# Layer 3 of a four-layer graph network: one of four sums over weights made by an accumulating transfer, weights made ten tiles ahead, a place of its own for the 13th pair

## The chip, the cores and the metric

The kernel runs on one core of one Trainium2 chip. The metric is the device time of an execution in microseconds. Before the change three runs took 2294.19, 2295.3 and 2300.17 us; their median is 2295.3 us.

## What is computed

The input is x (3327 rows of 256 numbers) and a 0/1 matrix adj (3327 by 3327). Four layers follow each other, each with a residual and a layer norm. Layer 3 is three attention layers in a row, called 3a, 3b and 3c here:

```python
def _gat_layer(h, adj, W, a):
    Wh = h @ W
    f1 = Wh @ a[:F_out]
    f2 = Wh @ a[F_out:]
    e = jax.nn.leaky_relu(f1 + f2.T, ALPHA)
    att = jnp.where(adj > 0, e, NEG_INF)
    att = jax.nn.softmax(att, axis=1)
    h_prime = att @ Wh
    return jax.nn.elu(h_prime)
...
h = input @ W0
h = _gat_layer(h, adj, W1, a1)
h = _gat_layer(h, adj, W2, a2)
h = _gat_layer(h, adj, W3, a3)
```

After them x = layernorm(x + h). All arithmetic is in 32-bit floats.

## The kernel before

The 3327 rows are padded to 3328: NT = 26 tiles of 128. The rows whose attention is computed are taken in NB = 7 blocks, six of 512 and one of 256. For one block the kernel runs over the 26 tiles of keys. For each tile it makes a 128 by 512 array of unnormalised weights, and TensorE multiplies these with the values of the tile, adding into PSUM.

**Weights.** In layer 3 (`Gat.weights`) a tile's weights need one ScalarE instruction (`re`, L787) and one VectorE instruction (L800), which also multiplies with the mask. For the blocks 0 to 5 L800 writes into the buffer FTA, seven groups of two rows of 512 numbers per partition. Three "quad" places of two groups each hold the weights of four tiles. `quad` (L702) hands the places out in turn, and counts seven quads to a block: six of four tiles and one for tiles 24 and 25, the 13th pair. The seventh group of FTA stays unused in layer 3.

**Products.** Two tiles make a pair, and a pair's product is made by Strassen's scheme (in Winograd's form) with seven products instead of eight (`products`, 28 matmuls at L935 for a pair and a block of 512). It needs four sums over the weights, s1 to s4, and four over the values (`tsums`). The sums over the weights are made on VectorE for two pairs at a time by `quad_sums` (L871 s3, L872 s1, L873 s2, L874 s4), each into a buffer of the pool "e", which has nine. The first pairs of block 0 and every 13th pair use `sums` (L883 to L886) instead. The sums over the values are made once (`combine`), stored to memory and fetched again for each block by `fetch_tsum` (L857, issued on SP's queue, three buffers); it is called when the weights of the pair are made.

**Order.** The loop goes over `steps` (layer, block, tile). At step s the weights are made up to `ahead_of`, in layer 3 seven tiles ahead (s + 3 + 4), fewer in block 0. In 3c's block 5 `extra` grows by one at each step from tile 11 on, so that the last block's weights are made early. `ahead` loads the row `u` of the next block (L774) and takes its exponential on ScalarE, from step `begin` on. Only the first steps are held to the written order. After that the order of the instructions on each engine is planned when the program is built; the written order counts as a priority there[...].

**Block start.** A block fills four of five PSUM banks. When a block is through, `joined` (L961 on ScalarE, L967 to L979 on VectorE) puts the seven products together and so frees the banks. The first bank of the next block is the fifth, the others have to come free. `finish` then normalises, transposes by a transfer (`turned`, L993), multiplies with the next layer's matrix (`pproj`, L1239), and in 3a and 3b makes the next layer's scores (L719) and sums over values.

**GpSimd** does little: in `combine` it sets a column of ones (`nc.gpsimd.memset`, L843), and once per layer it takes a maximum over partitions (L736).

Of the kernel before, what the change touches and what calls it, by code (L numbers as in the profile page):

```python
# [8 lines left out]
F32 = mybir.dt.float32  # L9
# [5 lines left out]
ALU = mybir.AluOpType  # L15
# [4 lines left out]
P = 128  # L20
D = 256
H = 128
LA = 2
CH = 512
ALPHA = 0.01
BETA = 1.0 - ALPHA
# [7 lines left out]
def gnn_stack(ctx: ExitStack, tc: tile.TileContext, a: dict, N: int, out: bass.AP):  # L34
# [8 lines left out]
    nc = tc.nc  # L43
    NT = (N + P - 1) // P
    NP = NT * P
    NB = (NP + CH - 1) // CH
    LASTP = N - (NT - 1) * P
    assert LASTP == P - 1

    def bw(b):  # L50
        return min(CH, NP - b * CH)

# [8 lines left out]
    work = ctx.enter_context(tc.tile_pool(name="work", bufs=2))  # L61
# [4 lines left out]
    def bank(name):  # L66
        return ps_b.tile([P, CH], F32, tag="pb", name=name)

# [14 lines left out]
    n = 8  # L83
# [19 lines left out]

    FTA = big.tile([P, NB, 2, CH], F32, name="ft")
    FT = [FTA[:, g] for g in range(NB)]
    QUADS = [FTA[:, 2 * r : 2 * r + 2].rearrange("p g h c -> p (g h) c") for r in range(3)]
# [196 lines left out]
    def load_xT(g):  # L303
        wd = bw(g)
        xT = work.tile([P, 2, CH], F32, tag="x4k", name="xT", bufs=2)
        src = a["xT"].rearrange("(h p) n -> p h n", p=P)
        if g == 0:
            for q, c in ((nc.scalar, 0), (nc.sync, D)):
                q.dma_start(xT[:, :, c : c + D], src[:, :, c : c + D])
        else:  # L310
            nc.sync.dma_start(xT[:, :, :wd], src[:, :, g * CH : g * CH + wd])
        xTs[g] = xT
# [108 lines left out]
    def mask(b, j, n=1):  # L421
        wd = bw(b)
        return masks[b][:, j * wd : (j + n) * wd]
# [183 lines left out]
    def by_pairs(L, b, p):  # L607
        return L.key == "2" and b < NB - 1 and p in (KPAIRS if b > 0 else (5, 7, 8, 10))
# [24 lines left out]
    def pair_weights(b, p):  # L633
# [38 lines left out]
        nc.vector.tensor_tensor(x[1][:, :D], c22, m45[:, :D], add)  # L672
        nc.vector.tensor_tensor(c22, c22, m45[:, D:], add)
        yield weights(1)
        m3 = two((s4, b22))
        nc.vector.tensor_tensor(c12, c12, m3[:, :D], add)  # L676
        yield weights(0)

    def weights2(b, j):
# [18 lines left out]

    def quad(i, b, j):
        return QUADS[((i * NB + b) * 7 + j // 4) % 3]  # L702

    class Gat:
        def __init__(self, key):
# [78 lines left out]
        def weights(self, b, j):  # L784
            wd = bw(b)
            t_ = work.tile([P, CH], F32, tag="a", name="re", bufs=4)
            nc.scalar.activation(  # L787
                t_[:, :wd],
                self.u[b][:, :wd],
                AF.Relu,  # L790
                bias=self.nrh[:, j : j + 1],
                scale=self.th[:, j : j + 1],
            )
            if self.quads and b < NB - 1:
                e = quad(self.quads, b, j)[:, j % 4, :]
            elif self.last and b == NB - 1:
                e = V[0][j]
            else:
                e = work.tile([P, CH], F32, tag="e", name="e", bufs=9)
            nc.vector.scalar_tensor_tensor(  # L800
                e[:, :wd],
                t_[:, :wd],
                self.rh[:, j : j + 1],
                mask(b, j),
                ALU.add,
                ALU.mult,
            )
            return e
# [6 lines left out]
    def strassen(L, b):  # L815
        if L.key == "0":
            return 0 < b < NB - 1
        if deep(L):
            return b < NB - 1
        return L.key == "2"  # L820

    def deep(L):
        return L.i > 2
# [3 lines left out]
    kept = {("0", 0): 1, ("0", 1): 1, ("0", 2): 1}  # L827
# [27 lines left out]
    def fetch_tsum(key, b, p):  # L855
        t = work.tile([P, 4 * H + 1], F32, tag="tsum", name="tsums", bufs=3)
        nc.sync.dma_start(t, t_d[key][p])  # L857
        tsums[b, p] = t
# [1 line left out]
    def two_slots(name):  # L860
        return [work.tile([P, 2, D], F32, tag="e", name=name, bufs=9) for _ in range(2)]

    def quad_sums(v):

        e11, e21, e12, e22 = (
            v[:, :, k, h * D : (h + 1) * D] for k in range(2) for h in range(2)
        )
        s3, s1, s2, s4 = (
            work.tile([P, 2, D], F32, tag="e", name="qsum", bufs=9) for _ in range(4)
        )  # L870
        nc.vector.tensor_tensor(s3, e11, e21, ALU.subtract)  # L871
        nc.vector.tensor_tensor(s1, e21, e22, ALU.add)  # L872
        nc.vector.tensor_tensor(s2, s1, e11, ALU.subtract)  # L873
        nc.vector.tensor_tensor(s4, e12, s2, ALU.subtract)  # L874
        return [tuple(x[:, a] for x in (e11, e12, e22, s1, s2, s3, s4)) for a in range(2)]

    def sums(b, e1, e2):

        hw = bw(b) // 2
        s3, s1, s2, s4 = (x[:, i, :hw] for x in two_slots("ssum") for i in range(2))  # L880
        e11, e21 = e1[:, :hw], e1[:, hw : 2 * hw]
        e12, e22 = e2[:, :hw], e2[:, hw : 2 * hw]
        nc.vector.tensor_tensor(s3, e11, e21, ALU.subtract)  # L883
        nc.vector.tensor_tensor(s1, e21, e22, ALU.add)
        nc.vector.tensor_tensor(s2, s1, e11, ALU.subtract)
        nc.vector.tensor_tensor(s4, e12, s2, ALU.subtract)  # L886
        return e11, e12, e22, s1, s2, s3, s4
# [593 lines left out]
    steps = [(L, b, j) for L in layers for b in range(NB) for j in range(NT)]  # L1481
    made = deque()

    pairs = {}

    def make(s):
        if s >= len(steps):
            return
        L, b, j = steps[s]
        make_weights(L, b, j)  # L1490
        if j % 2 and by_pairs(L, b, (j + 1) // 2):
            pairs[b, j + 1] = pair_weights(b, (j + 1) // 2)
            next(pairs[b, j + 1])

    cells = {}

    def in_quad(b, j):
        return j < NT - 2 and (b > 0 or j > 3)

    def make_weights(L, b, j):  # L1500
        if strassen(L, b) and j % 2 == 0 and kept.get((L.key, j // 2)) != b:
            fetch_tsum(L.key, b, j // 2)
        if by_pairs(L, b, j // 2):
            made.append(next(pairs[b, j - j % 2]))
            if j % 2:
                e1, e2 = made.pop(), made.pop()
                made.append(None)
                made.append(sums(b, e1, e2))
        else:
            if L.is_gat:  # L1510
                made.append(L.gat.weights(b, j))
                if deep(L) and strassen(L, b) and in_quad(b, j):
                    made[-1] = cells.setdefault((L.i, b, j // 2), []) if j % 2 else None
                    if j % 4 == 3:
                        v = quad(L.gat.quads, b, j).rearrange("p (a k) c -> p a k c", k=2)
                        for a_, x in enumerate(quad_sums(v)):
                            cells.pop((L.i, b, j // 2 - 1 + a_)).extend(x)
                    return
            else:
                made.append((weights0 if L.key == "0" else weights2)(b, j))  # L1520
            if strassen(L, b) and j % 2:
                e2, e1 = made.pop(), made.pop()
                made.append(None)
                made.append(sums(b, e1, e2))
# [15 lines left out]
    for part in (k0, q0, k0, q0, q0, k0, k0, q0, q1):  # L1540
        next(part, None)
    make(0)
    next(q1)
    make(1)
    prep = iter(())
    kprep = iter(())
# [3 lines left out]

    upto = LA
    extra = 0
    ends = deque()

    def make_to(n):
        nonlocal upto
        while upto < n:
            make(upto)
            upto += 1

    for s, (L, b, j) in enumerate(steps):
        last = L.key == "3c"
# [10 lines left out]
        if first:  # L1573
# [6 lines left out]
            elif j % 4 == 3 and j < 16:  # L1580
                load_xT((j + 9) // 4)
        ahead_of = s + LA + 1
        if deep(L):
            ahead_of += 4 if b else min(4, j // 3)
            if b == 0 and pending:
                ahead_of = max(s + LA + 1, min(ahead_of, L.i * NB * NT + NT - 2))
            if not last:
                end_of = (L.i + 1) * NB * NT
                ahead_of = max(s + LA + 1, min(ahead_of, end_of))
        make_to(ahead_of + extra)  # L1590
        if first:
            if j < 2:
                next(q1)
# [19 lines left out]
        if end:  # L1613

            k, h = divmod(2 * j, NT)
            for i in (h, h + 1):
                for o in range(2 if k else 1):
                    e = made[i][:, k * P : (k + 1) * P]
# [43 lines left out]
        if s == 3:  # L1662
            start.__exit__(None, None, None)
        if L.key == "0" and j == NT - 1 - LA:
            asum = sum_adj(b)
# [24 lines left out]
            nl, nb = (None if last else layers[L.i + 1]), 0  # L1690
        begin = 14
        if deep(L) and b < NB - 1:
            begin = 2 if last and b == NB - 2 else 10
        if L.key == "1" and (b, j) == (0, 22):
            sum_weights(w[L.w])
        if L.key == "2" and b * NT + j in KSTEPS:
# [91 lines left out]
```

## Time and profile before

| | value |
|---|---|
| median of three runs | 2295.3 us |
| the profiled execution, its own time | 2298.3 us |
| its span, first to last instruction | 2296.5 us |
| TensorE's granted clock, mean | 0.996 |
| ScalarE's L787, all | 728 instructions, 777 ns each |
| VectorE's L800 into ft | 468 instructions, 740 ns each |
| VectorE's L871, L872, L873, L874 | 105 each, 681 ns median |
| TensorE's L935 from tsums and qsum | 2520 records, 277 ns each |
| transfers, total | 286.13 MB, mean 125 GB/s |

The profile comes from one execution, which took 2298.3 us where the median of the runs is 2295.3. A long name such as `po<-tsums,qsum` says what is written and from what. A matmul in 32-bit floats leaves two records. Matmuls overlap, so their mean durations are longer than the steps from one to the next; the same holds for VectorE, where a row's 681 ns stand for about 0.60 us from start to start in the timeline. A wait is put down to the release that the profile saw last, which is not always the operand that was really missing.

Layer 3 begins at about 1368 us, where L800 writes its first ft (1369.6 us), and lasts to the end.

### The profile page before, as it was taken

How to read it: one execution, taken by the hardware profiler on the slowest of the kernel's cores; microseconds unless marked ns; L12 is line 12 of the kernel's file. 1: busy time of each engine (PE TensorE's matmuls, PEld its weight loads, DVE VectorE, ACT ScalarE, POOL GpSimd, SP SyncE). 2: the span in 40 equal slices, each digit the busy share in tenths (PEclk: the TensorE clock that was granted, in tenths of full speed). 3: DMA queues.
4: the chain of work that ended last, by engine and by line, in shares of the span. 5: the costliest groups of instructions: out<-in, count | busy, mean ns of one | idle time of the engine just before them, and what ended most of it. 6: DMA issues, size and time to landing. Idle time of an engine off the chain costs nothing.

```text
span 2296.5 us, 41597 instructions
## 1 busy us (share of the span) xinstructions
PE 2253.7 (98%) x15183; PEld 2004.9 (87%) x15183; DVE 1982.4 (86%) x5407; ACT 1239.4 (54%) x2012; POOL 41.6 (2%) x196
## 2 busy tenths in 40 slices
PE   9999999999999999999999999999999999999997
PEld 7788887888888877888888899999999999999997
DVE  7789999866777777898898889899799998899996
ACT  4667777764555423223233245666666665665763
POOL 0000001000000000000000000000000000000000
PEclk9999999999999999999999999999999999999999
DMA  8655565523222322132132254454444544355542
GB/s 277 196 177 177 188 193 188 162 84 90 77 72 55 106 62 80 56 100 81 56 100 71 74 176 127 131 151 130 122 122 143 136 143 137 95 165 155 154 120 56
DMA packets 186207, 286.13 MB, mean 125 GB/s; under 512 B 80413, under 2 KB 105492, under 8 KB 181396
## 3 DMA queue, kind: packets, MB, share of 16 engines
q1 hardware_dynamic: 185732, 283.22, 41.2%
q8 instruction: 120, 1.97, 0.4%
q14 instruction: 83, 0.68, 0.1%
q10 hardware_dynamic: 272, 0.26, 0.1%
HBM read 228.21 MB, written 38.44 MB: 116 GB/s over the span
## 4 chain that ended last, share of the span: by engine, by line
PE 75%; DVE 14%; DMA 4%; ACT 4%; issue 2%; POOL 0%; DVEq 0%; SPq 0%; ACTq 0%; POOLq 0%
PE po L935 35%; PE po L1653 16%; PE ps L647 6%; PE ps L511 6%; PE ps L686 5%; DVE ft L800 3%; DMA turned<-planes 2%; PE pproj L1239 2%; ACT re L787 2%; DVE qsum L873 1%; DVE qsum L872 1%; DVE ejunk L719 1%; PE pv L1322 1%; PE pgq L541 1%; DVE qsum L874 1%
## 5 line engine op out<-in xcount | busy, mean ns | idle before, releaser
L787 ACT ACTIVATE re<-u,nrh,th 128x512 f32<-128x512 f32 (+1 forms) x728 | 536.6, 777 | 348.1 <-DVE ft L800 172.9
L1653 PE MATMUL po<-v,e 128*128 128x257 f32 x1872 | 422.3, 381 | 1.0 <-ACT p L1182 0.8
L1653 PEld LDWEIGHTS po<-v,e 128*128 128x128 f32 x1872 | 353.0, 190 | 60.5 <-issue 9.8
L935 PE MATMUL po<-tsums,qsum 128*128 128x128 f32 (+1 forms) x2520 | 353.9, 277 | 15.8 <-ACT re L787 9.2
L800 DVE SCALAR_TENSOR_TENSOR ft<-re,rh,mask 128x512 f32<-128x512 f32 x468 | 339.1, 740 | 16.1 <-ACT re L787 14.2
L935 PEld LDWEIGHTS po<-tsums,qsum 128*128 128x128 f32 x2520 | 317.2, 193 | 19.1 <-ACT re L787 12.8
L935 PE MATMUL po<-tsums,ssum 128*128 128x128 f32 (+1 forms) x2082 | 292.5, 276 | 3.8 <-DMA tsums<-t3a_d 1.9
L935 PE MATMUL po<-v,ft 128*128 128x129 f32 x1872 | 287.6, 277 | 4.1 <-DVE p L975 3.4
L935 PEld LDWEIGHTS po<-tsums,ssum 128*128 128x128 f32 x2082 | 262.3, 192 | 6.3 <-DMA tsums<-t3a_d 2.3
L935 PEld LDWEIGHTS po<-v,ft 128*128 128x128 f32 x1872 | 252.9, 193 | 9.7 <-issue 5.0
L935 PEld LDWEIGHTS po<-v,e 128*128 128x128 f32 x1196 | 172.4, 192 | 37.6 <-issue 24.9
L935 PE MATMUL po<-v,e 128*128 128x129 f32 x1196 | 185.1, 275 | 0.0
L800 DVE SCALAR_TENSOR_TENSOR e<-re,rh,mask 128x512 f32<-128x512 f32 (+1 forms) x234 | 148.9, 655 | 38.4 <-PE po L1653 28.3
L524 ACT ACTIVATE ex<-ps,rq 128x512 f32<-128x512 f32 (+1 forms) x183 | 118.8, 652 | 114.8 <-PE ps L511 112.0
L511 PE MATMUL ps<-ft 128*128 128x512 f32 (+1 forms) x364 | 166.9, 564 | 0.0
L496 DVE SCALAR_TENSOR_TENSOR e<-ex,mask 128x512 f32<-128x512 f32 (+1 forms) x182 | 115.4, 648 | 48.9 <-ACT ex L694 31.6
L525 DVE SCALAR_TENSOR_TENSOR e<-ex,mask 128x512 f32<-128x512 f32 (+1 forms) x183 | 116.6, 643 | 32.4 <-ACT ex L524 32.0
L935 PE MATMUL po<-tsums,ft 128*128 128x128 f32 x936 | 143.1, 275 | 0.0
L686 PE MATMUL ps<-gT,ft 128*128 128x512 f32 (+1 forms) x336 | 129.8, 527 | 0.0
L935 PE MATMUL po<-v,qsum 128*128 128x128 f32 x840 | 128.4, 275 | 0.0
L935 PEld LDWEIGHTS po<-tsums,ft 128*128 128x128 f32 x936 | 123.6, 192 | 0.0
L660 ACT ACTIVATE ex<-ex,off 128x512 f32<-128x512 f32 x98 | 67.0, 716 | 101.7 <-DVE ex L676 69.1
(347 smaller groups left out, 3566.0 us busy)
## 6 DMA issues: line engine op xcount, KB each, us to landing
mask<-mask_d SPq DMA_DIRECT2D x30, 1664.0 KB
stage<-in_adj_a SPq DMA_DIRECT2D x78, 512.0 KB
tsums<-t_d SPq DMA_DIRECT2D x152, 256.5 KB
tsums<-t3a_d SPq DMA_DIRECT2D x77, 256.5 KB
tsums<-t3b_d SPq DMA_DIRECT2D x77, 256.5 KB
tsums<-t3c_d SPq DMA_DIRECT2D x77, 256.5 KB
mask_d<-mask SPq DMA_DIRECT2D x6, 1664.0 KB
u<-s_d SPq DMA_DIRECT2D x24, 256.0 KB
```

The costliest lines, as they stand in the source:

```text
L496: nc.vector.scalar_tensor_tensor(e[:, :wd], t_[:, :wd], 0.0, mask(b, j), ALU.add, ALU.mult)
L511: nc.tensor.matmul(ps[:, :wd], FT[j // 4][:, 0, (j % 4) * P : (j % 4 + 1) * P], FT[b][:, 1, :wd], start=True, stop=True,)
L524: nc.scalar.activation(t_[:, c], ps[:, c], AF.Exp, scale=rq[:, j : j + 1])
L525: nc.vector.scalar_tensor_tensor(e[:, c], t_[:, c], 0.0, mask(b, j)[:, c], ALU.add, ALU.mult)
L647: nc.tensor.matmul(ps[:, i * D : (i + 1) * D], l, r, start=True, stop=True)
L660: nc.scalar.activation(x[k], x[k], AF.Exp, bias=off, scale=1.0 / D**0.5)
L686: nc.tensor.matmul(ps[:, :wd], FT[j // 4][:, h, (j % 4) * P : (j % 4 + 1) * P], g[:, h, :wd], start=(h == 0), stop=(h == 1),)
L787: nc.scalar.activation(t_[:, :wd], self.u[b][:, :wd], AF.Relu, bias=self.nrh[:, j : j + 1], scale=self.th[:, j : j + 1],)
L800: nc.vector.scalar_tensor_tensor(e[:, :wd], t_[:, :wd], self.rh[:, j : j + 1], mask(b, j), ALU.add, ALU.mult,)
L935: nc.tensor.matmul(o, x, y, start=(p == 0 and g not in banks[:i]), stop=(p == NT // 2 - 1 and g not in banks[i + 1 :]),)
L1239: nc.tensor.matmul(pm[:, :D], pT[:, h, :], w[L.w][:, h, :], start=(h == 0), stop=(h == 1),)
L1653: nc.tensor.matmul(pos[k], e[:, k * P : (k + 1) * P], V[L.i % 2][i], start=(i == 0), stop=(i == NT - 1),)
```

## The change

Six things are changed, all for 3a, 3b and 3c.

1. `quad_sums` writes s1 over e21, the part of the weights that only s1 and s3 read, instead of taking a fourth buffer. In most quads (all of the blocks 1 to 5, and from tile 15 on in block 0) s1 isn't made on VectorE: GpSimd's queue issues a transfer that adds e22 onto e21 in place. In the other quads VectorE makes it in place.
2. The function becomes a generator. In the queued quads s2 and s4, which need s1, are made only when the weights of three more tiles have been made (`SLACK`, `due`, `make_due`), at the latest with tile 25.
3. `quad` gives tiles 24 and 25 the seventh group of FTA, and the six quads of a block go over the three places in turn.
4. The weights are made s + LA + 9, that is up to ten tiles further than the step's own need, in the blocks from 1 on; in block 0 the lead grows with j // 2 instead of j // 3. In block 5 of each layer and in the last block there are limits of their own.
5. `fetch_tsum` is no longer called with the weights: `fetch_to` calls it at most six tiles ahead of the step.
6. `begin`, the step from which `ahead` runs, goes from 10 to 6.

```diff
-    def quad(i, b, j):
-        return QUADS[((i * NB + b) * 7 + j // 4) % 3]
+    def quad(j):
+        if j >= NT - 2:
+            return FTA[:, NB - 1]
+        return QUADS[j // 4 % 3]
...
-    def quad_sums(v):
+    def quad_sums(v, queued):
...
-        s3, s1, s2, s4 = (
-            work.tile([P, 2, D], F32, tag="e", name="qsum", bufs=9) for _ in range(4)
-        )
+        qsum = lambda: work.tile([P, 2, D], F32, tag="e", name="qsum", bufs=9)
+        s3, s1 = qsum(), e21
         nc.vector.tensor_tensor(s3, e11, e21, ALU.subtract)
-        nc.vector.tensor_tensor(s1, e21, e22, ALU.add)
+        if queued:
+            nc.gpsimd.dma_start(out=s1, in_=e22, accum_op=ALU.add)
+            yield
+        else:
+            nc.vector.tensor_tensor(s1, e21, e22, ALU.add)
+        s2, s4 = qsum(), qsum()
         nc.vector.tensor_tensor(s2, s1, e11, ALU.subtract)
         nc.vector.tensor_tensor(s4, e12, s2, ALU.subtract)
-        return [tuple(x[:, a] for x in (e11, e12, e22, s1, s2, s3, s4)) for a in range(2)]
+        yield [tuple(x[:, a] for x in (e11, e12, e22, s1, s2, s3, s4)) for a in range(2)]
...
+    fetched = 0
+
+    def fetch_to(n):
+        nonlocal fetched
+        while fetched <= min(n, len(steps) - 1):
+            L, b, j = steps[fetched]
+            if strassen(L, b) and j % 2 == 0 and kept.get((L.key, j // 2)) != b:
+                fetch_tsum(L.key, b, j // 2)
+            fetched += 1
...
         L, b, j = steps[s]
+        if not deep(L):
+            fetch_to(s)
         make_weights(L, b, j)
+        make_due(j)
...
+    due = deque()
+
+    def make_due(j):
+
+        if due and j >= due[0][0]:
+            _, (i, b, p), rest = due.popleft()
+            for a_, x in enumerate(next(rest)):
+                cells.pop((i, b, p + a_)).extend(x)
...
-                        v = quad(L.gat.quads, b, j).rearrange("p (a k) c -> p a k c", k=2)
-                        for a_, x in enumerate(quad_sums(v)):
-                            cells.pop((L.i, b, j // 2 - 1 + a_)).extend(x)
+                        v = quad(j).rearrange("p (a k) c -> p a k c", k=2)
+                        queued = b > 0 or j > 11
+                        rest = quad_sums(v, queued)
+                        if queued:
+                            next(rest)
+                        k = min(j + SLACK, NT - 1) if queued else j
+                        due.append((k, (L.i, b, j // 2 - 1), rest))
...
-            ahead_of += 4 if b else min(4, j // 3)
+            far = s + LA + 9
+            plain = (L.i * NB + NB - 1) * NT
+            if b == NB - 2:
+                far = min(far, max(ahead_of + 4 + extra, plain))
+            elif b == NB - 1:
+                far = ahead_of + 4 + extra
+            ahead_of = far if b else min(far, ahead_of + j // 2)
...
-        make_to(ahead_of + extra)
+        if deep(L):
+            fetch_to(min(s + LA + 4, ahead_of - 1))
+        make_to(ahead_of)
...
-            begin = 2 if last and b == NB - 2 else 10
+            begin = 2 if last and b == NB - 2 else 6
```

More of the change, by code (lines that the diff above doesn't have):

```diff
@@ L23 @@
 LA = 2
+SLACK = 3
 CH = 512
@@ L794, in weights @@
             if self.quads and b < NB - 1:
-                e = quad(self.quads, b, j)[:, j % 4, :]
+                e = quad(j)[:, j % 4, :]
             elif self.last and b == NB - 1:
@@ L1500, in make_weights @@
     def make_weights(L, b, j):
-        if strassen(L, b) and j % 2 == 0 and kept.get((L.key, j // 2)) != b:
-            fetch_tsum(L.key, b, j // 2)
         if by_pairs(L, b, j // 2):
```

## The prediction

> **What bounds the kernel now.** I read the page's busy shares first, then busy time by stretch, then the waits of the matmul engine, then the timeline at two block starts, one with a hole and one without.
>
> ```profile
> PE 2253.7 (98%) x15183; PEld 2004.9 (87%) x15183; DVE 1982.4 (86%) x5407; ACT 1239.4 (54%) x2012; POOL 41.6 (2%) x196
> ...
> core 0: us, PE busy (x) PEld busy (x) DVE busy (x) ACT busy (x) POOL busy (x), PEclk, DMA share, GB/s
> 1376.00:2122.00 746.00, 722.30 (x5930) 703.23 (x5928) 691.10 (x1639) 466.75 (x743) 3.67 (x30) 1.00 0.47 135
> 2122.00:2264.00 142.00, 141.56 (x1171) 138.72 (x1172) 135.74 (x335) 90.61 (x138) 0.00 (x0) 1.00 0.47 132
> ```
>
> TensorE is the bound. The change touches only layer 3, about 1368 us to the end. From 1376 to 2122 us TensorE stands 746.0 - 722.3 = 23.7 us; in the last blocks of 3c (2122 to 2264) it stands 0.4 us. The prize is therefore some 24 us, 1% of the span, unless the matmuls themselves change, and the diff leaves all of them.
>
> ```profile
> PE po L935 <- ACT re L787: 9.2, 7, 2.4
> PE po L935 <- DVE p L975: 3.4, 6, 1.0
> PE po L935 <- DMA tsums<-t3a_d: 2.3, 3, 1.5
> PE po L935 <- DVE zs L970: 2.2, 1, 2.2
> PE po L935 <- issue: 2.2, 2, 1.9
> ...
> 1603.82 0.61 PE L935 MATMUL po<-v,ssum 128*128 128x128 f32 x4
> 1604.27 0.83 PE L935 MATMUL po<-v,ft 128*128 128x129 f32 x6
> 1607.53 0.77 PE L935 MATMUL po<-tsums,qsum 128*128 128x128 f32 x2 [2.43 <-ACT re L787]
> ...
> 1605.69 0.68 DVE L872 TENSOR_TENSOR qsum<-ft 128x512 f32<-128x512 f32 x1
> 1606.30 0.15 DVE L967 COPY zs<-po 128x2 f32<-128x2 f32 x1
> 1606.41 0.69 DVE L873 TENSOR_TENSOR qsum<-qsum,ft 128x512 f32<-128x512 f32 x1
> ...
> 1607.15 0.28 DVE L973 TENSOR_TENSOR p<-p,po 128x128 f32<-128x128 f32 x1
> ...
> 2208.57 0.83 PE L935 MATMUL po<-v,ft 128*128 128x129 f32 x6
> 2209.24 1.06 PE L935 MATMUL po<-tsums,qsum 128*128 128x128 f32 x8
> ```
>
> The waits name ACT re, but the operand had been ready for long. Six matmuls of the new block go into the fifth PSUM bank, the seventh needs a bank of the old block, and it starts at 1607.53, just after L973 of joined() (the first ends at 1607.43) has read that bank. So the hole is VectorE and ScalarE coming late to joined(): L967 starts 2.0 us after the new block's first matmul. At 2208.57 it was early (VectorE's L967 at 2208.17 in the timeline) and there is no hole. Adding up the holes of the timeline between 1372 and 2265 us that stand at such block starts (2.23, 1.47, 0.81, 2.43, 1.67, 1.62, 1.44, 2.77, 1.87, 0.87, 0.23) gives 17.4 us; the rest is 4.5 us at layer starts and the last blocks, 1.1 us of tsums fetches and small ones.
>
> Why is VectorE late? From 1588.75 to 1607.7 it works almost without a pause (0.6 us), and its row of weights (L800) is bound by places: block 5 of 3a starts its first weight at 1593.89, when the matmuls of tiles 16 to 19 are through in block 4, because pair 13 takes a whole quad place and the third place back is theirs. That is six tiles before the block start; its weights, the sums of the quads and the follow-up of hidden layers all fall into the same 10 us.
>
> **What the Trainium skill says.** "DMA: Bandwidth & Descriptors", section "SWDGE vs HWDGE vs iDMA": an accumulating transfer can be issued from GpSimd alone, its descriptors written in software. Section "Anatomy of one DMA — SWDGE (gpsimd) path": about 2.0 us fixed plus bytes over 436 GB/s; for 256 KB an estimate of 2.6 us, for a plain copy. The trace has no GpSimd transfer; its nearest rows are SP's: a 256.5 KB store issued at 1589.70 releases VectorE at 1593.68 (4.0 us), a 256 KB load of u issued at 1581.78 releases ScalarE at 1585.07 (3.3 us), and tsums pieces in the chain of waits run up to 8.05 us beside a mask load. "SBUF — State Buffer", section "Who interferes with whom": tensor_tensor has no two-port mode and does not lock GpSimd's writes out; no run so far shows it.
>
> **The change part by part.**
> - *Sum by transfer.* Per layer, queued quads are 5 blocks x 6, and j = 15, 19, 23 of block 0: 33, in three layers 99. Each takes an L872 off VectorE, 681 ns long, 0.60 us from start to start: 99 x 0.60 = 59 us of VectorE, 3.6 us per block. Of the stretch between 1588.75 and 1607.43 three L872 go (1588.75, 1599.97, 1605.69): 1.8 us of the 2.4 us hole. Elsewhere the time buys nothing, as TensorE is the bound.
> - *What it adds.* 99 transfers of 256 KB on GpSimd's queue, 26 MB on top of 286 (the destination is read as well). The DMA engines are 0.47 busy, so it is room enough on average; beside a mask load (one per block) it is late. GpSimd is 2% busy; ahead of a transfer in its queue can stand the memset of the ones column (L843), which waits for an x4k place, but the VectorE subtraction behind the same place waits as well.
> - *The added wait.* s2 waits for the landing. Behind it on VectorE's queue stand weights, other sums and, at a block start, joined(), for which TensorE waits within 0.7 us. Three tiles later is 3 x 0.66 = 2.0 us if VectorE runs flat out and 3 x 1.56 = 4.7 us at TensorE's pace. Latency unknown: bounds 2.6 us (the page) and 8 us (the longest piece above); I take 4.5 us, the store's 4.0 plus something for the read of the destination. Then the landing is in time at TensorE's pace and late by up to 2.5 us in a burst. The instruction order is planned with a modelled latency (L852 of one pair stands between two sums of another), so other work will stand in most of these gaps. A mean stall of 0.5 us would cost 99 x 0.5 = 50 us of VectorE, less than the 59 removed; a gain below nothing is not excluded and is the rival below.
> - *Place for pair 13, ten tiles ahead.* Six quads over three places: quad 0 of the next block follows quad 3 and starts ten tiles ahead of the block start instead of six, 4 x 1.56 = 6 us earlier. It spreads the burst and makes room for late sums: +0 to -5 us, counted with the holes. The mask is no obstacle: it is issued at 1586.37 for a block whose weights start at 1643.50, just after the last weight of two blocks earlier (1585.59) has freed its buffer. u is loaded from step 6 instead of 10, which the lead needs; its 3.3 us lie beside matmuls.
> - *One place of nine less per quad* (s1 lies in e21) and the two DVE sums of block 0 in place: 0.
> - *fetch_to.* tsums are fetched at most six tiles ahead, and three buffers allow no more anyway (SP waits for po 428 us in L857 now): 0, without it the lead would block SP's queue. With 3a's first pairs fetched from step 0 on: +0 to 1.5 us (a hole of 1.5 us on tsums is there now).
> - *Last block.* Its weights come later in program order; VectorE does them from 2232.97 on, with nothing else urgent: 0 to +1 us.
>
> Sum: three quarters of the 17.4 us at block starts, -13; half of 2.5 us of holes on sums elsewhere, -1; new waits at some of 18 block starts, +3: -11 us. What is late next is the PSUM bank itself: ScalarE's copy (0.35), L967 to L973 (0.4) against six matmuls (0.67), and the 3c blocks show this fits. The profiled execution took 2298.3 us (span 2296.5) and becomes 2287; the median of the runs, 2295.3, becomes 2284.
>
> **The rivals.**
> - *A: holes stay.* In 3c (2122 to 2264) VectorE is busy 95.6% and TensorE does not stand; before 2122 it is busy 92.6% and TensorE does. So it may be order, not load: ScalarE's weights ahead of its copy L961 (1605.86, behind one at 1605.14), or the wait for the transposed tile on ScalarE (2.55 us at 1575.72). Then a fifth of the 17.4 goes: -3 us, 2292. Against it: from 1588 on VectorE has no pause.
> - *B: slower, VectorE stands at the head of its queue for the accumulate.* Its place: s2 (L873), 99 times. VectorE's spare per quad is the 0.6 us removed and 0.4 us of today's idle (746 - 691 = 55 us over about 80 queued quads is 0.7, part of it unusable). It decides from a latency of about 3.0 (flat out, with another sum between) + 1.0 + 0.5 = 4.5 us if the plan puts nothing else in between, close to what I take; each 0.25 us more costs 99 x 0.25 = 25 us, as TensorE then waits for sums. With 4.75 us: 2320. For it: traffic at 0.47 and loads of up to 8 us. Against: the lead of ten tiles is 15.6 us, and a plan that knows the latency.
> - *C: it doesn't do what it says*: the lead is not reached because re or places are late; then it goes like A.
>
> **How the numbers follow.** Forecast, 2284 (2276 to 2289 by the unknowns): 0.56. A and C, 2292: 0.17. B, 2320 (2296 to 2380): 0.27. No change means within 0.3%, about 7 us, what a measurement of this kernel can tell (2288.4 to 2302.2). Faster: 0.53 of the forecast and 0.03 of A, 0.56; same: 0.03 + 0.14 + 0.02 = 0.19; slower 0.25. The range from 2275 leaves 0.05 out below, and up to 2316 about 0.15 of B above.
>
> **What would show it.** L872 falls from 105 to 6; L873 shows no long wait for a DMA; the stretch that is now 746 us has under 13 us of TensorE idle; the L935 waits for re, p and zs fall from 15 us to under 5; L800 of a block starts ten tiles ahead. Wrong: VectorE idle before L873 on a landing, over 0.5 us a quad, and TensorE waiting for qsum; or joined() still 2 us late with VectorE on time.

## The result, and the profile after

The changed kernel took 2518.0 us, median of four runs (2508.7 to 2528.6); the kernel before, run beside it, took 2294.7 us. The ratio is 1.097, interval 1.092 to 1.102. The forecast was 2284 us, the range ended at 2316 us, and slower had been given 0.25. The profiled execution took 2528.6 us, its span is 2526.8 us; the profile shown of the kernel before has a span of 2296.5 us. Lines have moved: s3 is now L873, the transfer L875, s2 L880, s4 L881, the weights L803 (ScalarE's part L790), the products L942.

The page of the changed kernel, rows of the parts on busy time, slices, queues, groups and transfers:

```profile
PE 2323.2 (92%) x15183; PEld 2066.9 (82%) x15183; DVE 1940.0 (77%) x5308; ACT 1243.3 (49%) x2012; POOL 161.3 (6%) x295
...
PEclk9999999999999999999999998999988989988998
...
q0 software_dynamic: 26928, 25.96, 7.1%
...
L942 PE MATMUL po<-tsums,qsum 128*128 128x128 f32 x1680 | 251.2, 296 | 109.3 <-ACT re L790 60.8
...
L880 DVE TENSOR_TENSOR qsum<-ft 128x512 f32<-128x512 f32 x105 | 72.5, 691 | 258.6 <-DMA ft<-ft 253.0
...
L875 POOL DMA_DIRECT2D ft<-ft x99 | 119.1, 1204 | 744.0 <-DVE qsum L873 343.7
...
ft<-ft POOLq DMA_DIRECT2D x99, 256.0 KB, 4.5
```

The row of s2 and the row of the clock before:

```profile
L873 DVE TENSOR_TENSOR qsum<-qsum,ft 128x512 f32<-128x512 f32 x105 | 71.5, 681 | 0.5
...
PEclk9999999999999999999999999999999999999999
```

VectorE does 42 us less work than before (1940.0 against 1982.4) and the span is 230 us longer. The row of L880 says where: its 105 instructions are busy for 72.5 us, and before them VectorE stood 258.6 us, where it stood 0.5 us before. Of these, 253.0 us ended with the landing of a transfer. The median transfer takes 4.5 us from issue to landing. The row PEclk shows a second loss: the granted clock of TensorE drops in seven of the last sixteen slices.

The same stretches as in the prediction, by busy time:

```profile
core 0: us, PE busy (x) PEld busy (x) DVE busy (x) ACT busy (x) POOL busy (x), PEclk, DMA share, GB/s
1376.00:2122.00 746.00, 621.42 (x4724) 602.07 (x4723) 518.32 (x1230) 375.06 (x598) 82.53 (x93) 0.92 0.53 129
2122.00:2264.00 142.00, 119.45 (x898) 115.36 (x897) 106.46 (x253) 75.61 (x120) 16.16 (x16) 0.92 0.56 139
```

Of 746 us, TensorE stands 125 us (24 before) and VectorE 228 us (55 before). With both idle for so long, neither is the bound: the time goes into a wait that VectorE sits out at the head of its queue. The clock of 0.92 is a mean; the clock record of the trace has full and half speed only.

The difference of the spans, 2526.8 - 2296.5 = 230.3 us, divides on TensorE into 160.8 us of more idle time (203.6 against 42.8, span less busy) and 69.5 us of more busy time (2323.2 against 2253.7) for the same 15183 matmul records.

Where it happens, on VectorE's timeline in 3b (start, duration, engine, line; in brackets the idle time before):

```profile
2010.78 0.69 DVE L873 TENSOR_TENSOR qsum<-ft 128x512 f32<-128x512 f32 x1
2011.38 1.41 DVE L803 SCALAR_TENSOR_TENSOR ft<-re,rh,mask 128x512 f32<-128x512 f32 x2
2015.96 0.69 DVE L880 TENSOR_TENSOR qsum<-ft 128x512 f32<-128x512 f32 x1 [3.18 <-DMA ft<-ft]
...
2019.17 0.68 DVE L873 TENSOR_TENSOR qsum<-ft 128x512 f32<-128x512 f32 x1
...
2024.66 0.41 DVE L1270 SCALAR_TENSOR_TENSOR v<-elu_e,z 128x256 f32<-128x256 f32 x1
2030.06 0.69 DVE L880 TENSOR_TENSOR qsum<-ft 128x512 f32<-128x512 f32 x1 [4.98 <-DMA ft<-ft]
```

On GpSimd's and on SP's queue beside it:

```profile
2011.99 1.20 POOL L875 DMA_DIRECT2D ft<-ft  x1 [5.49 <-DVE qsum L873]
2020.39 1.20 POOL L875 DMA_DIRECT2D ft<-ft  x1 [7.19 <-PE po L942]
```

```profile
2020.54 0.32 SPq L428 DMA_DIRECT2D mask<-mask_d  x1
```

In the first quad shown, s3 is followed on VectorE's queue by two weights (2011.38 to 2012.78) and then by s2. The transfer went out at 2011.99 and landed 4 us later, so VectorE stood 3.18 us. In the second, the last of a block, fifteen other instructions stood between the two, until 2025.1; but the load of the next block's mask (1664 KB) went out 0.15 us after the transfer, and s2 could start only 9.7 us after the issue. Over all 99 transfers the trace gives 3.7 us at least, 4.5 us as the median, 5.4 us as the mean; 16 took over 8 us, up to 11.3. Each of these 16 has a mask load that was issued between 2.0 us before it and 1.2 us after it.

The whole sum can be read from the start and landing times of the 99 transfers. From the end of s3 it takes 0.6 us on average until the transfer is issued and 5.4 us until it has landed. VectorE has 3.4 us of other work there (1.3 to 5.4 us), so about 2.5 us are left, 99 times. The 16 late ones make up 95 us of the stand before s2.

"Perfetto Trace Analysis" in the Trainium skill, section "Tensor Engine Instruction (MATMUL, LD_WEIGHTS)", calls the queues of VectorE and ScalarE strictly first in, first out. The trace agrees for VectorE, as ScalarE's timeline shows:

```profile
2012.16 1.52 ACT L790 ACTIVATE re<-u,nrh,th 128x512 f32<-128x512 f32 x2 [0.41 <-DVE ft L803]
2017.36 0.81 ACT L790 ACTIVATE re<-u,nrh,th 128x512 f32<-128x512 f32 x1 [3.68 <-DVE ft L803]
```

Two more `re` were made by 2013.7, but the weights that use them stood behind s2 and came after 2016.5. ScalarE then stood 3.68 us, until such a weight had freed a place for `re`. So a stall of VectorE is not made good by work done in advance meanwhile: ScalarE stops with it.

What follows on TensorE, from its own timeline:

```profile
2018.92 1.06 PE L942 MATMUL po<-tsums,qsum 128*128 128x128 f32 x8
...
2039.79 0.37 PE L768 MATMUL psr<-ident,sd 128*4 128x128 f32 x1 [6.65 <-DVE sd L722]
...
2053.41 2.05 PE L942 MATMUL po<-tsums,qsum 128*128 128x128 f32 x8 [3.88 <-ACT re L790]
2055.25 0.64 PE L942 MATMUL po<-v,ft 128*128 128x129 f32 x2
2055.68 1.92 PE L942 MATMUL po<-tsums,ft 128*128 128x129 f32 x8
```

TensorE stands 6.65 us for a score that VectorE makes, and 3.88 us at the next block start. Then eight records of the kind that took 1.06 us at 2018.92 take 2.05 us. (Where matmuls are counted, 28 to a pair, the trace's records are meant; the kernel issues 14 for a pair.) "TensorE: Matmul & The Clock Gate" in the Trainium skill, section "Part 1: The HAM clock gate (the "warmup" mystery)", states that after an idle window of about 3.4 us the array runs at half its clock. The trace agrees in part. Its clock record has 32 stretches at half the clock, 195 us of the span, nearly all of 3.4 or 6.8 us; before there were three, 16.8 us. Apart from the stretch at the very end of the kernel, 23 of them began in or just after a gap of TensorE of 3.4 us or more, but eight at gaps of only 1.9 to 3.3 us, and the two before at gaps of 2.2 and 2.4 us. Here the measurement decides: shorter gaps than the page's can be followed by the half clock. TensorE was busy for 137.8 us of these stretches, 6.6 us before. Half of the difference, 66 us, is an estimate of what the slow clock cost, and close to the 69.5 us of additional busy time.

TensorE's waits for fetched sums over values (`tsums`) grow as well, from 2.7 us between 1376 and 2264 us before to 32.2 us.

### The profile page after: what moved, and what is told of

It is laid out like the page before. It is cut to its first block, busy times and chain, and to the rows that moved or that the text cites. A ratio compares the mean times of both kernels' runs of the same rounds, so it can differ in the third digit from the quotient of the medians.

```text
span 2526.8 us, 41544 instructions
## 1 busy us (share of the span) xinstructions
PE 2323.2 (92%) x15183; PEld 2066.9 (82%) x15183; DVE 1940.0 (77%) x5308; ACT 1243.3 (49%) x2012; POOL 161.3 (6%) x295
## 5 line engine op out<-in xcount | busy, mean ns | idle before, releaser
L790 ACT ACTIVATE re<-u,nrh,th 128x512 f32<-128x512 f32 (+1 forms) x728 | 540.4, 778 | 590.6 <-DVE ft L803 337.8
L803 DVE SCALAR_TENSOR_TENSOR ft<-re,rh,mask 128x512 f32<-128x512 f32 x468 | 336.6, 744 | 31.1 <-PE po L942 26.1
L942 PE MATMUL po<-tsums,qsum 128*128 128x128 f32 x1680 | 251.2, 296 | 109.3 <-ACT re L790 60.8
L942 PEld LDWEIGHTS po<-tsums,qsum 128*128 128x128 f32 x1680 | 227.8, 209 | 115.5 <-ACT re L790 62.5
L942 PE MATMUL po<-v,ft 128*128 128x129 f32 x1872 | 302.5, 286 | 3.8 <-DVE p L982 3.0
L942 PE MATMUL po<-tsums,ssum 128*128 128x128 f32 (+1 forms) x2082 | 292.3, 276 | 2.0 <-DVE ssum L892 1.4
L942 PE MATMUL po<-tsums,ft 128*128 128x128 f32 (+1 forms) x1776 | 261.2, 291 | 28.7 <-DMA ft<-ft 26.6
L942 PEld LDWEIGHTS po<-v,ft 128*128 128x128 f32 x1872 | 266.8, 202 | 9.2 <-issue 3.4
L880 DVE TENSOR_TENSOR qsum<-ft 128x512 f32<-128x512 f32 x105 | 72.5, 691 | 258.6 <-DMA ft<-ft 253.0
L942 PEld LDWEIGHTS po<-tsums,ssum 128*128 128x128 f32 x2082 | 262.2, 192 | 4.3 <-DVE ssum L892 2.0
L942 PEld LDWEIGHTS po<-tsums,ft 128*128 128x128 f32 x1776 | 239.2, 207 | 30.9 <-DMA ft<-ft 28.0
L942 PEld LDWEIGHTS po<-v,e 128*128 128x128 f32 x1196 | 172.4, 191 | 37.9 <-issue 24.7
L942 PE MATMUL po<-v,e 128*128 128x129 f32 x1196 | 185.2, 275 | 0.1
L803 DVE SCALAR_TENSOR_TENSOR e<-re,rh,mask 128x512 f32<-128x512 f32 (+1 forms) x234 | 148.9, 655 | 36.7 <-PE po L1691 28.1
L875 POOL DMA_DIRECT2D ft<-ft x99 | 119.1, 1204 | 744.0 <-DVE qsum L873 343.7
L942 PE MATMUL po<-v,qsum 128*128 128x128 f32 x840 | 136.5, 288 | 0.0
```

The costliest lines, as they stand in the source:

```text
L790: nc.scalar.activation(t_[:, :wd], self.u[b][:, :wd], AF.Relu, bias=self.nrh[:, j : j + 1], scale=self.th[:, j : j + 1],)
L803: nc.vector.scalar_tensor_tensor(e[:, :wd], t_[:, :wd], self.rh[:, j : j + 1], mask(b, j), ALU.add, ALU.mult,)
L875: nc.gpsimd.dma_start(out=s1, in_=e22, accum_op=ALU.add)
L942: nc.tensor.matmul(o, x, y, start=(p == 0 and g not in banks[:i]), stop=(p == NT // 2 - 1 and g not in banks[i + 1 :]),)
```

## The experiments

Theory 1 is the mechanism of rival B: s2 waits at the head of VectorE's queue for the landing, and everything behind it waits with it. Against it stood three others: that the order of places, lead and fetches is spoilt (rival 2 in the expectations); that the 26 MB of transfers or their issue disturb other work (rival 3); that the three-tile delay does. The medians and the ratios to runs of the kernel before on the same chip:

| kernel | us | ratio, interval |
|---|---|---|
| e1, all sums on VectorE, rest of the change kept | 2306.3 | 1.0045, 1.0033 to 1.0057 |
| e2, s2 taken from s3, transfers kept | 2314.6 | 1.0078, 1.0066 to 1.0090 |
| e3, the last quad of each block on VectorE | 2420.9 | 1.0540, 1.0523 to 1.0558 |
| e4, five tiles of delay for three | 2397.4 | 1.0432, 1.0412 to 1.0452 |
| e5, kernel before with transfers, s2 from s3 | 2297.2 | 1.0005, 0.9997 to 1.0013 |
| e6, kernel before with transfers and their wait | 2456.5 | 1.0694, 1.0678 to 1.0709 |
| e7, e2 with priority for `joined` | 2315.8 | 1.0088, 1.0074 to 1.0102 |
| e7b, kernel before with priority for `joined` | 2292.0 | 0.9987, 0.9980 to 0.9995 |
| e9, e5 with block 0 on VectorE | 2299.6 | 1.0016, 1.0010 to 1.0023 |
| e10, e9 with priority for `joined` | 2296.1 | 1.0003, 0.9995 to 1.0011 |
| e11, e2 with the old lead and `begin` | 2317.9 | 1.0092, 1.0077 to 1.0108 |
| e12, e5 with the own place for pair 13 | 2316.7 | 1.0092, 1.0078 to 1.0105 |
| e13, e2 without the delay | 2315.5 | 1.0089, 1.0076 to 1.0103 |

### Without transfers (e1), and with transfers that s2 doesn't wait for (e2)

```diff
-                        queued = b > 0 or j > 11
+                        queued = False
```

> The changed kernel, but s1 always made in place by VectorE, no transfer; lead of ten tiles, place for the 13th pair, fetch_to and begin stay. Theory 1 (VectorE stands in its queue at L880 until the accumulate has landed, 253 us in all): the loss is gone, 2285 to 2298 us, no wait of VectorE on a landing of ft. Rival 2 (the new order of places, lead or fetches costs the time): still above 2400 us. Rival 3 (the transfers' traffic or GpSimd's issue costs it): as theory 1 here.

Since s1 = e21 + e22 and s3 = e11 - e21, s2 = s1 - e11 is also e22 - s3. e2 writes it so; only the matmuls read s1 then.

```diff
-        nc.vector.tensor_tensor(s2, s1, e11, ALU.subtract)
+        nc.vector.tensor_tensor(s2, e22, s3, ALU.subtract)
```

> The changed kernel with one operand pair changed: s2 = e22 - s3 instead of s1 - e11, the same number, so that no VectorE instruction needs the transfer; the 99 transfers stay. Theory 1: 2278 to 2300 us, and TensorE alone waits for a landing now and then. Rival 3 (traffic, issue on GpSimd): 2450 us or more. Rival 2: 2450 us or more.

e1 came to 2306.3 us, so nearly all of the loss hangs on the transfers; it is some 8 us above what was expected of it, a remainder that the other parts of the change cost. e2 keeps all 99 transfers and comes to 2314.6 us: 203 of the 223 us are gone with one operand changed. That is 15 us above what was expected, a remainder that is taken up below. The row of s2 and the stretch by busy time in e2:

```profile
L880 DVE TENSOR_TENSOR qsum<-ft,qsum 128x512 f32<-128x512 f32 x105 | 71.9, 685 | 0.8
```

```profile
1376.00:2122.00 746.00, 719.23 (x5903) 698.05 (x5903) 649.27 (x1544) 466.25 (x744) 103.47 (x113) 1.00 0.67 163
```

The idle time before s2 is 0.8 us for 258.6, TensorE is at full clock again, and the DMA engines are busier than in the changed kernel (0.67 against 0.53). TensorE's waits for tsums are back at 1.9 us. In e2, too, 13 of the 99 landings take over 8 us, and no instruction of VectorE waits for them. It was not the traffic, it was who waited for it.

### The collision with the mask (e3) and more cover (e4)

```diff
-                        queued = b > 0 or j > 11
+                        queued = (b > 0 or j > 11) and j < 23
```

> The changed kernel, with the sixth quad of each block (j = 23) left to VectorE: 81 transfers instead of 99. These are the transfers that start within a microsecond of a mask load and land after 9 to 11 us. Theory 1 with the mask as a large part of it: 18 stalls of about 5 us go, 2518 becomes 2420 to 2450 us. If the mask has no special part: a sixth of the loss goes, about 2480 us. Rival 2: no change.

```diff
-                        k = min(j + SLACK, NT - 1) if queued else j
+                        k = min(j + (5 if b else SLACK), NT - 1) if queued else j
```

> The changed kernel with five tiles instead of three between s3 and s2 in the blocks from 1 on: in VectorE's built order 12.2 instructions stand between them on average instead of 7.9. Theory 1: 4.3 x 0.6 = 2.6 us more cover for each transfer, VectorE's wait at L880 falls from 253 us to 60 to 130 us, the time to 2360 to 2430 us. Rivals 2 and 3: 2500 us or more.

The waits of VectorE in e3 and e4 (total, times, longest):

```profile
DVE qsum L880 <- DMA ft<-ft: 159.8, 67, 5.1
```

```profile
DVE qsum L880 <- DMA ft<-ft: 98.6, 38, 7.0
```

With the last quad of each block back on VectorE, 18 of 99 transfers are gone and 97 us with them; no landing takes over 8 us any more. So the sixth quads, a fifth of the transfers, make over 40% of the loss. What is left is as telling: the 81 landings of e3 take 4.5 us on average, and VectorE still stands 159.8 / 81 = 2.0 us for each. With two tiles more of delay the wait falls to 98.6 us in total and the time by 121 us. In the built program, the number of instructions on VectorE's queue between s3 and s2 goes from a mean of 7.9 (most often 2, in 28 of 105 quads) to 12.2. Both came out as theory 1 expected, and both fit a loss that is set by the latency less the work between s3 and s2.

### The transfer in the kernel before, with its wait (e6) and without (e5)

e6 puts `quad_sums`, SLACK and `make_due` into the kernel before and leaves its places, its lead and its `begin`; `fetch_to` comes with it.

> The change's transfer alone: s1 by transfer, s2 after it and three tiles later, but lead, places of the quads and begin as before the change. In VectorE's built order 7.6 instructions stand between s3 and s2 on average, 7.9 in the changed kernel. Theory 1 (VectorE waits in its queue for the landing): nearly the whole loss, 2450 to 2550 us, with 200 us or more of VectorE's wait at s2. If the lead of ten tiles or the places make the waits what they are: under 2400 us.

e5 is the kernel before with its buffers as in the change (s1 in e21) and these lines:

```diff
-        nc.vector.tensor_tensor(s1, e21, e22, ALU.add)
-        nc.vector.tensor_tensor(s2, s1, e11, ALU.subtract)
+        if queued:
+            nc.gpsimd.dma_start(out=s1, in_=e22, accum_op=ALU.add)
+        else:
+            nc.vector.tensor_tensor(s1, e21, e22, ALU.add)
+        nc.vector.tensor_tensor(s2, e22, s3, ALU.subtract)
```

> The kernel before, with s1 by transfer in the same 99 quads and s2 = e22 - s3, so that VectorE waits for no transfer; lead and places as before. It takes 59 us off VectorE and adds the traffic. If the holes at block starts come from VectorE's load (the step of the prediction): 2280 to 2288 us. If they come from the order of the queues: 2293 to 2303 us, with VectorE's share falling to about 87% and TensorE's idle unchanged.

e6: 2456.5 us, 160 us above the kernel before: the waiting transfer alone does most of the harm, and the place and the lead, which were to make room for it, add 61 us to that. The waits of VectorE in e6, then one of its transfers on GpSimd's queue and the mask on SP's:

```profile
DVE qsum L878 <- DMA ft<-ft: 210.5, 89, 7.4
```

```profile
1522.90 1.20 POOL L873 DMA_DIRECT2D ft<-ft  x1 [6.58 <-issue]
```

```profile
1525.41 0.32 SPq L428 DMA_DIRECT2D mask<-mask_d  x1
```

Here the mask load goes out 2.5 us after the sixth quad's transfer, at other blocks mostly 1.2 to 2.5 us after it, and only 3 landings take over 8 us, for 16. The mask's buffer comes free with the weights of tile 25; with a place of its own, pair 13 follows the sixth quad at once, and the mask with it. That is the reading that fits both timelines, and e12 below bears it out.

e5: 2297.2 us, no change. The relief of VectorE does arrive (its share falls to 84%), but not in the time. That is in the range expected if the order of the queues makes the holes, and yet the holes do shrink. The waits of TensorE between 1376 and 2264 us in e5:

```profile
PE po L937 <- DMA ft<-ft: 5.6, 3, 2.0
PE po L937 <- DVE p L977: 3.7, 10, 0.9
PE pproj L1241 <- DVE zlast L1388: 2.5, 1, 2.5
PE po L937 <- ACT re L787: 2.4, 2, 1.3
```

The holes at block starts (re, p) fall to 6 us, where the prediction counted 17.4. Three new ones take 5.6 us: the quad at tile 15 of block 0, once in each layer, where the lead is short and the matmuls reach s1 before it has landed. And the end (the row of zlast, here 2.5 us, 0.8 before) grows: from the start of the last block of 3c to the end e5 takes 46.6 us for 43.4. The span is 3.5 us shorter in the profiled execution (2293.0 against 2296.5); over 13 runs nothing of it is left. Of the two profiled executions, e5's was faster than its median, 2294.7 against 2297.2 us, and the one before slower, 2298.3 against 2295.3 us.

### What the other 20 us are (e12, e11, e13, e7)

e12 is e5 with only `quad` as in the change (three lines); e11 is e2 with the lead and `begin` of before (`fetch_to` stays, at the same distance of six tiles); e13 is e2 with s2 and s4 made at once; e7 is e2 with a priority for `joined`:

```diff
# e11
-            far = s + LA + 9
...
+            ahead_of += 4 if b else min(4, j // 3)
# e13
-                        k = min(j + SLACK, NT - 1) if queued else j
+                        k = j
# e7
-                z = joined(pos, b, p4)
+                with tc.high_priority():
+                    z = joined(pos, b, p4)
```

> e5_before_free (transfer, nobody on VectorE waiting, lead as before) with one part of the change added: the place of its own for the 13th pair, so that a block's first weights can begin ten tiles ahead of it. If this place lets weights stand ahead of joined() and so costs what separates e11 (2318 us) from e5 (2297 us): 2308 to 2318 us. If it is the three tiles' delay of s2 and s4 or the fetches: 2294 to 2301 us.

> e2_s2_from_s3 with the lead, fetches and begin as before the change; the place for the 13th pair stays. e2 is 17 us over e5, which has neither. If the lead of ten tiles (more weights and sums ahead of joined() in the queues) costs it: 2294 to 2302 us. If the place costs it: 2308 to 2316 us.

> e2_s2_from_s3 (transfer, nobody on VectorE waiting, lead of ten tiles, own place) with s2 and s4 made at once instead of three tiles later. If the delay is what costs e2 its 17 us over e5: 2294 to 2301 us. If the place or the lead: 2309 to 2316 us.

> e2_s2_from_s3 with a higher priority for joined() in the planned order, so that fewer weights and sums stand ahead of it on VectorE and ScalarE at a block start. If the place of joined() in the queues makes the holes: 2295 to 2305 us, waits of L942 on re and p under half of the 18 us of e2. If not: 2310 to 2318 us.

Neither the lead (2317.9) nor the delay (2315.5) nor the rank of `joined` (2315.8) moves e2's 2314.6 us. The place alone does: from 2297.2 to 2316.7 us (2296.3 and 2295.8 us for the kernel before beside them). Waits of TensorE between 1376 and 2264 us in e12, and VectorE at one of its block starts:

```profile
PE po L939 <- DVE p L979: 9.0, 13, 0.8
PE po L939 <- DMA ft<-ft: 7.7, 4, 2.2
PE po L939 <- ACT re L789: 5.4, 6, 1.4
PE po L939 <- issue: 4.1, 5, 1.3
```

```profile
1823.93 0.68 DVE L872 TENSOR_TENSOR qsum<-ft 128x512 f32<-128x512 f32 x1
1824.53 0.15 DVE L971 COPY zs<-po 128x2 f32<-128x2 f32 x1
...
1825.38 0.69 DVE L877 TENSOR_TENSOR qsum<-ft,qsum 128x512 f32<-128x512 f32 x1
1825.99 0.41 DVE L978 TENSOR_TENSOR p<-p,po 128x256 f32<-128x256 f32 x1
...
1826.40 0.66 DVE L878 TENSOR_TENSOR qsum<-ft,qsum 128x512 f32<-128x512 f32 x1
1826.98 0.41 DVE L979 TENSOR_TENSOR p<-p,po 128x256 f32<-128x256 f32 x1
```

L971 to L979 are part of `joined`. The sums of a new quad (L872 s3, L877 s2, L878 s4) fall exactly there, one ahead of it and two inside it, and TensorE then waits for L979. The row for p has thirteen such waits, none over 0.8 us: the same hole at nearly every block start from 1521 us on. That makes 12.4 us more at block starts than in e5 (9.0 + 5.4 + 4.1 against 3.7 + 2.4), 2.1 us more for landings, 1.1 us more at zlast, and 3.8 us more of busy matmuls, of 22.3 us between the two spans. With seven quads on three places the phase between quads and block starts changes from block to block; with six on three it is the same in every block, and it is a bad one. That is read from the timeline; no run shifted the phase to prove it, and why e7 did not cure it stays open. Nor did a run put the place alone into the kernel before: in e1, where place, lead, fetches and `begin` of the change stand without any transfer, they cost 9 us together, so part of the 19.5 us comes from place and transfers together.

The place alone also moves the mask load. In e5 the mask load nearest to a transfer mostly goes out 3 to 5 us after it, and no landing takes over 8 us. In e12 it mostly goes out 1.1 us ahead of the transfer, as here, and 10 landings take over 8 us:

```profile
1497.20 0.32 SPq L427 DMA_DIRECT2D mask<-mask_d  x1
1498.31 1.20 POOL L874 DMA_DIRECT2D ft<-ft  x1 [6.93 <-PE po L939]
```

### Looking for a version that gains (e7b, e9, e10)

> The kernel before with a higher priority for joined() alone. If the place of joined() in the queues makes the holes at block starts (17 us): 2283 to 2291 us. If VectorE's load makes them: 2293 to 2299 us.

> e5_before_free, but block 0 of each layer makes all its s1 on VectorE: 90 transfers instead of 99. In e5 the holes at block starts are 6 us instead of 17, and TensorE waits 5.6 us for the landings at tile 15 of the three blocks 0, where the lead is short. If these waits gave the gain back: 2288 to 2293 us, and no wait of TensorE on a landing of ft. If VectorE's relief has no worth: 2295 to 2300 us.

> e9_free_b1 with the higher priority for joined() of e7b, which by itself gave 0.13%. If both add up: 2283 to 2290 us, faster than the kernel before beyond the interval. If both work on the same holes: as e9_free_b1.

e9 (`queued` only for b > 0) takes the 5.6 us of waits for landings out of e5 and should have gained them; it came to 2299.6 us over 21 runs. In its profile other waits of TensorE are longer than in e5: for tsums by 2.8 us and, of `pproj` for ScalarE, by 2.9 us. e10 adds the priority: 2296.1 us. The priority for `joined` in the kernel before, with no transfer at all, gives 2292.0 us over 17 runs, 0.9987 (0.9980 to 0.9995): the one version ahead of both kernels, and by less than the 0.3% that were set as the limit of a change. It lies between what was expected if the place of `joined` in the queues makes the holes (2283 to 2291 us) and if VectorE's load does (2293 to 2299 us), so it settles neither.

## Why the prediction was wrong

**The step that failed** is the price of the added wait. The prediction put it so: "The instruction order is planned with a modelled latency (L852 of one pair stands between two sums of another), so other work will stand in most of these gaps. A mean stall of 0.5 us would cost 99 x 0.5 = 50 us of VectorE, less than the 59 removed". The stall is 253.0 / 99 = 2.56 us. The cover was too small: VectorE had 3.4 us of work between s3 and s2 on average, and in the most frequent case two instructions, about 1.4 us, not the 4.7 us of three tiles at TensorE's pace. One observed case of work between two sums was taken for a rule. In e3 the landings take what the prediction took, 4.5 us on average, and the stall is still 2.0 us. The latency of 4.5 us was right as the median only. The 0.6 us from s3's end to the issue was put at nothing, and the 16 landings beside a mask load, about 10 us each, were left out of the mean; e3 puts 97 us of the loss on the sixth quads. e2 (one operand, 203 us back) and e4 (more cover, 121 us back) show that the wait is the cause.

**The rival with the right mechanism was too small.** B named the place and the wait, and got 2320 us from a latency 0.25 us above its limit. Three terms were missing in it. It let three tiles and another sum cover 3 us, and gave VectorE credit for spare time that lies elsewhere. The prediction knew that a transfer beside a mask load is late, but not that the own place for pair 13 makes the mask go out beside nearly every sixth quad (e3: 97 us). And B ended with VectorE: after TensorE's gaps its own work takes longer (69.5 of the 230.3 us).

**Removing 59 us from VectorE** happened: no add on VectorE is left in 99 quads, and VectorE's busy time fell by 42 us in the changed kernel and by 49 us in e5 (1982.4 to 1933.2). The estimate of what it buys was high: with the wait gone (e5) the block-start holes fall by 11 us, close to the 13 counted, but there are new waits of 5.6 us for landings in block 0 and of some 3 us at the end. The prediction had 3 us of new waits, at block starts, and at most 1 us at the end. So even without the stall the forecast of 2284 us would have been missed: e5 gives 2297.2 us.

**Own place and ten tiles ahead, "+0 to -5 us"**: the wrong sign for the place. Added to transfers that s2 doesn't wait for, it costs 19.5 us (e12), and through the mask it makes the wait dearer. "The mask is no obstacle" looked at when the mask is needed, not at what else is on the way when it is sent. The lead costs and brings nothing measurable beside that place (e11 against e2).

**Right were** TensorE as the bound with some 24 us to gain, the traffic as harmless on average (e2 and e5 at a DMA share of 0.67), and the signs named in advance for being wrong: VectorE idle before s2 on a landing over 0.5 us a quad, and TensorE waiting behind it. The fetches were put at nothing; no run takes `fetch_to` alone, and where nothing waits for a transfer, in e2, TensorE's waits for tsums are no longer than before.

## What to carry to other kernels

Work handed from an in-order engine to a transfer is only gone if no instruction of that engine waits for the landing: count the instructions that the built order really puts between issue and wait, and where they are few, rewrite the arithmetic (here s2 = e22 - s3) so that only a consumer with a long lead reads the result. Price a wait of two microseconds or more on TensorE twice, once as idle time and once for what it can do to TensorE's clock. And a buffer place that changes the rhythm of a ring moves every load that is tied to it; look at what then goes out at the same moment.

## What the hardware showed that had not been expected

An accumulating transfer of 256 KB within SBUF, issued by GpSimd, holds GpSimd's queue for 1.20 us and lands 3.7 us after issue at the earliest, 4.5 us as the median, and 9 to 11 us after issue when a mask load goes out within half a microsecond after it (13 such transfers in the changed kernel). The 2.6 us that the prediction worked out from "DMA: Bandwidth & Descriptors", section "Anatomy of one DMA — SWDGE (gpsimd) path", for a plain copy were never reached; the measurement decides. Gaps of 1.9 to 9.1 us went with 31 stretches of TensorE at half its clock, in which eight matmul records took 2.05 us where they had taken 1.06 us.
